# A state-space scan with side work planned into it: one product moved a step later, matmul allowance held back before GpSimd tiles, and two products per image moved from GpSimd to VectorE

## The chip, the cores and the metric

The kernel runs on one core of a Trainium2 chip. The core has a matmul engine (TensorE, PE), a vector engine (VectorE, DVE), an activation engine (ScalarE, ACT), a general-purpose engine (GpSimd, POOL) and SyncE (SP), which here only issues DMAs. Each engine runs its own instructions in order and waits for the others by semaphores. PE writes to PSUM, a small memory that DVE and ACT can read[...]. The metric is the device time of one execution in microseconds (us).

## What is computed

The input x is 8 images of 64 x 64 pixels with 96 channels. The first layer is a normalisation, two projections, a 3 x 3 depthwise convolution, and then a selective scan over all 4096 pixels of an image in four directions, whose results are added and gated. The second layer is a multilayer perceptron between an up- and a downsampling, written as matrix products. Nearly all the time belongs to the scan:

```python
K, D_INNER, D_STATE = 4, 192, 16
def step(h, inp):
    ul, dl, Bl, Cl = inp
    dA = jnp.exp(dl[..., None] * A)
    h = dA * h + (dl * ul)[..., None] * Bl[:, :, None, :]
    y = jnp.einsum('bkdn,bkn->bkd', h, Cl)
    return (h, y)
_, ys = lax.scan(step, h0, (u_t, d_t, B_t, C_t))
return y + xs * Dk[None, :, :, None]
...
y = (y1 + y2 + y3 + y4)
```

For each of 192 channels and 16 states there is one recurrence h = dA * h + (dl * u) * B along the pixels. The sum over the 16 states of h * C is y. The four directions k differ in the order in which they go through the pixels. All numbers are float32.

## The kernel before

**Tiles and chunks.** A tile is 8 channels with 16 states each, so 128 partitions, times 1024 pixels. 24 tiles make a chunk (all 192 channels of 1024 pixels), 4 chunks a direction, 4 directions (in the order k = 1, 0, 2, 3) an image, so an image has 16 chunks, c0 to c15, and the program 3072 tiles. The 24 tiles of a chunk fall into three thirds q of 8 tiles. Chunk c1 is the second chunk of direction k = 1.

**A tile's work**, in the order of dependence:

- `fetch` (L1020): a DMA on SP brings dl * u, spread over the 16 states, into `dub` (4 buffers).
- `product_b` (L1026): POOL multiplies it by B: `bb` (4 buffers).
- `decay` (L1032, L1039): PE spreads dl over the states into a PSUM tile `pd` (2 buffers), ACT takes the exp in place.
- `scan` (L1046): DVE runs the recurrence over `pd` and `bb`. The result goes back into `pd`, or, for a tile that has `by_pool` set, into `h` in SBUF[...].
- `product_c` (L1052): the product with C, on DVE, or on POOL for a tile with `by_pool`: every third tile of a chunk (tiles 2, 5, 8, ... 23).
- `hold` (L1065): the last state is copied into `carry` for the next chunk; on ACT for a tile with `by_pool`, on DVE otherwise. It is left out in a direction's last chunk.
- `sums` (L1084): for each pair of tiles, PE adds the 16 states up into the PSUM tile `py`, which gathers a whole third and has one buffer.

When a third is complete, one more PE product (L1096) adds to `py` what `before` has loaded as `yp`: for k = 1 it is u times a diagonal matrix of D, for k = 2 and 3 the result of an earlier direction. k = 0 has no such product. Then `store` copies `py` to `yq` on ACT (L1117) and, one turn later, writes it with two DMAs on SP (L1120).

**The order** of all engines' instructions is written out by hand (`tc.manual_schedule()`), one turn of the loop at L1143 per tile, called step i here, and counted within its chunk (0 to 23) in what follows. Step i issues, in this order: the load of `yp` if tile i is the fifth of its third (L1180), the fetch of tile i + 6, the POOL product C of tile i - 1 if that tile is POOL's, the product B of tile i + 3, the decay of tile i + 1, the scan of tile i with its DVE product C and its carry, then side work (`side.advance`, L1197), at times a filler matmul (`turn_over`, L1054), and in odd steps the sums of tiles i - 3 and i - 2. So the last sums of a third, and the product L1096 behind them, stand in steps 1, 9 and 17 of a chunk; those in step 1 belong to the last third of the chunk before.

**Side work** is all the rest: the first layer's front for the next image, the tail of the last image's scan, its multilayer perceptron, and for the next chunk the projections and dl (`prepare`). It is written as generators. Each piece says what it will cost before it is issued: us of an engine, KB of DMA, and PSUM banks. The planner, `Side`, gives each step an allowance per engine (L49: for PE 2.2 us, and with what is saved at most 2.9), and `emit` issues a piece only if its allowance is left. `advance` goes through stores, then urgent pieces, then the rest. Its argument `taken` is PE time that the step will use for itself: 0.95 us for a pair's sums and 0.95 for the product L1096. `turn_over` issues a filler matmul (L1058) when the step has spent less than 1.0 us of PE.

The parts of the side work that come up below are: `tail`'s sum of two directions on POOL (`ty`, L646), the upsampling copies on ACT (`t1s`, L769, two buffers) with their writes on SP (L775), and the load `u` (L933) with which `prepare` begins, in step 16 of most chunks.

Of the kernel before, what the change touches and what calls it, by code (L numbers as in the profile page):

```python
# [25 lines left out]
NT = DI // 8  # L26
# [11 lines left out]
class Side:  # L38
# [66 lines left out]
            active.append(entry)  # L105
        return True

    def advance(self, caps, more=1, spare=1, taken=0.0):

        self.caps, self.spent = caps, taken
        if caps:
            self.left = {e: min(self.left.get(e, 0.0) + c, most) for e, (c, most) in caps.items()}
            self.left["pe"] -= taken
        self.free += self.given
        self.given = []
        for active, spare_ in ((self.stores, 0), (self.hurried, 0), (self.active, spare)):  # L120
            for entry in list(active):
                if not self.emit(entry, spare_):
                    active.remove(entry)
            for _ in range(2):
                if self.urgent and active is self.hurried:
                    self.start(self.urgent, self.hurried, 0)
        for _ in range(more):
            if not self.queue or not self.start(self.queue, self.active, spare):
                break

    def drain(self):
        while self.stores or self.urgent or self.hurried or self.queue or self.active:
            self.advance(None, more=2)
# [3 lines left out]
def kernel(ctx: ExitStack, tc: tile.TileContext, a: dict, out: bass.AP):  # L137
    nc = tc.nc
# [13 lines left out]
    def load(name, shape, pool=cp):  # L152
        t = pool.tile(shape, F32, tag=name, name=name)
        queue().dma_start(t, a[name])
        return t

    ident = load("ident", [128, 128])
# [55 lines left out]
    d_diag = cp.tile([128, Q3, 128], F32, name="d_diag")  # L213
# [6 lines left out]
    with tc.tile_pool(name="ps0", bufs=1, space=PSUM) as ps0, tc.tile_pool(name="setup", bufs=1) as c0p:  # L220
# [76 lines left out]
        for quarter in range(2):  # L297
            grid = wave[:, cols[SIDE, quarter]]
            start, stop = quarter == 0, quarter == 1
# [4 lines left out]
                start=start,  # L304
                stop=stop,
                skip_group_check=True,
            )
        for quarter in range(2):
            grid = wave[:, cols[SIDE, quarter]]
            start, stop = quarter == 0, quarter == 1  # L310
# [50 lines left out]
    side = Side(pss)  # L361
# [636 lines left out]
    tiles = []  # L998
    for b in range(images):
        for k in (1, 0, 2, 3):  # L1000
            order = range(NCH) if k < 2 else range(NCH - 1, -1, -1)
            for n, c in enumerate(order):
                got = {}
                for i in range(NT):
                    q, n8 = divmod(i, 8)
                    s, j = n8 % 2, n8 // 2
                    tiles.append(
                        dict(b=b, k=k, i0=c * T, first=n == 0, i=i, q=q, s=s, j=j, g=8 * q + 4 * s + j, got=got)
                    )
                    tiles[-1]["last"] = n == NCH - 1  # L1010
                    tiles[-1]["by_pool"] = i % 3 == 2
    carry = pp.tile([128, NT], F32, tag="carry", name="carry", bufs=1)

    summed = set()
# [60 lines left out]
    def sums(two):  # L1075

        t0 = two[0]
        if t0["j"] == 0:
            t0["got"]["py"] = psy.tile([128, MB], F32, tag="py", name="py")
        py = t0["got"]["py"]  # L1080
        for t in two:
            for hf in range(2):
                r0 = 64 * hf + 32 * t["s"]
                nc.tensor.matmul(  # L1084
                    py[r0 : r0 + 32],
                    sel_r[:, t["j"], :],
                    t["hc"][:, MB * hf : MB * hf + MB],
                    start=(t["j"] == 0),
                    stop=(t["j"] == 3 and t["k"] == 0),
                    skip_group_check=True,  # L1090
                )

        if t0["j"] == 3 and t0["k"]:

            add = d_diag[:, t0["q"], :] if t0["k"] == 1 else ident
            nc.tensor.matmul(py, add, t0["got"]["yp"], start=False, stop=True, skip_group_check=True)  # L1096

    def before(t):

# [14 lines left out]
    def store(t):  # L1114
        yield dict(act=0.7)
        yq = sp.tile([128, MB], F32, tag="yq", name="yq", bufs=1)
        nc.scalar.copy(yq, t["got"]["py"])  # L1117
        yield {}
        for hf, part in enumerate(parts(t)):
            nc.sync.dma_start(part, yq[64 * hf : 64 * hf + 64])  # L1120
        if t["q"] == Q3 - 1:
            if t["k"] == 3:
                summed.add((t["b"], t["i0"] // T))
            elif t["k"] == 2 and t["i0"] == 0:
                summed.add((t["b"], "even"))
# [3 lines left out]
    with tc.manual_schedule():  # L1129
        side.queue, rest = front(0)  # L1130
        side.drain()
        side.urgent = prepare(0, tiles[0]["k"], tiles[0]["i0"], tiles[0]["got"])
        side.drain()
        n = len(tiles)
        for i in range(FETCH):
            fetch(tiles[i])
            if i >= FETCH - LEAD:
                product_b(tiles[i - FETCH + LEAD])
        decay(tiles[0])
        begin, *side.later = prepare(0, tiles[NT]["k"], tiles[NT]["i0"], tiles[NT]["got"])  # L1140
        side.urgent.append(begin)
        total = 1
        for i in range(n + 4):  # L1143
            t = tiles[i] if i < n else None
            at = i % (NT * NCH * K)
            if t and t["i"] == 0:
                b = t["b"]
                if at == 0:
                    y_dram[b] = [dr.tile([DI, L], F32, tag=f"y{o}", name=f"y{o}") for o in range(2)]
                    side.begun, hasty = 0, sum(item[1] for item in rest) if b == 0 else 0  # L1150
                    side.queue += rest
                    down, end = [], []
                    if b:
                        keep = {}
                        side.queue += tail(b - 1, keep)
                        up, down, end = mlp(b - 1, keep)
                        side.queue += up
                    if b + 1 < images:
                        start, rest = front(b + 1)
                        side.queue += start[:2] + [i for two in zip(down, start[2:10]) for i in two] if b else start[:10]  # L1160
                        side.queue += start[10:] + rest
                        rest = []
                    else:
                        side.queue += down
                    side.queue += end
                    total = sum(item[1] for item in side.queue)
                if b == images - 1 and at == NT * NCH * (K - 1):
                    keep = {}
                    side.queue += tail(b, keep, pairs=False)
                    total = 0  # L1170

            ahead = 4 if i < 2 * NT else 8
            if (i + ahead) % NT == 0 and i + ahead + NT < n:
                nxt = tiles[i + ahead + NT]
                begin, *side.later = prepare(nxt["b"], nxt["k"], nxt["i0"], nxt["got"])
                side.urgent.append(begin)
            if i % NT == 0:
                side.urgent += side.later
                side.later = []
            if t and t["i"] % 8 == 4:  # L1180
                before(t)
            if i + FETCH < n:
                fetch(tiles[i + FETCH])
            if 0 < i <= n and tiles[i - 1]["by_pool"]:
                product_c(tiles[i - 1])
            if i + LEAD < n:
                product_b(tiles[i + LEAD])
            if i + 1 < n:
                decay(tiles[i + 1])
            if t:  # L1190
                scan(t)
                if not t["by_pool"]:
                    product_c(t)
                hold(t)
            ends = i % 2 == 1 and 3 <= i <= n + 2
            adds = ends and tiles[i - 2]["j"] == 3 and tiles[i - 2]["k"]
            side.advance(  # L1197
                Side.CAPS,
                2 if not total or side.begun < max(hasty, total * at / 290) else 0,
                0 if 7 <= i % NT <= 21 else 1,  # L1200
                0.95 * (bool(ends) + bool(adds)),
            )
            turn_over()
            if ends:
                sums(tiles[i - 3 : i - 1])
                if tiles[i - 2]["j"] == 3:
                    side.stores.append([g := store(tiles[i - 2]), next(g)])
        up, down, end = mlp(images - 1, keep)
        side.queue += up + down + end
        side.drain()  # L1210
# [89 lines left out]
```

## Time and profile before

| | us |
|---|---|
| median of 3 runs | 11214.56 |
| lowest and highest of them | 11200.23, 11256.48 |
| the profiled execution's own time | 11227.57 |
| its span | 11225.8 |

The page's groups, each a line of the code on one engine, show what a tile costs:

| group | count | mean ns | idle before, us in total |
|---|---|---|---|
| L1026 POOL, product B | 3072 | 2359 | 254.7 |
| L1052 POOL, product C | 1024 | 2357 | 370.8 |
| L1052 DVE, product C | 2048 | 1225 | 157.2 |
| L1046 DVE, scan into pd, with carry | 1536 | 2350 | 287.7 |
| L1046 DVE, scan into h, with carry | 768 | 2339 | 7.8 |
| L1046 DVE, scan into pd, first chunks | 512 | 2291 | 149.5 |
| L1039 ACT, exp | 3072 | 1087 | 4592.7 |

Matmuls are better read from the timeline, where one merged row is a group of them: the decay of a tile is 1.13 us, the sums of a pair 1.07, the product L1096 1.13, a filler 1.13. "Idle before" is the time for which the engine did nothing before the rows of this group; it is a loss only where the engine is the one that sets the pace. In the timeline it stands in brackets behind the row, with the instruction that ended it: `[1.76 <-ACT carry L1065]` means that the engine had stood still for 1.76 us until an ACT instruction, by semaphore the one at L1065, released it. If several instructions of that engine end within a short time, the name may be that of a neighbour.

The first scan starts 142.5 us into the span, the last one ends at 10930.8; what follows is the multilayer perceptron of the last image. An image takes 1334 to 1360 us, most chunks take 79 to 92 us.

### The profile page before, as it was taken

Reading aid. Unit: us, or ns where it says so; the run is one execution under the profiler, and the core shown is the slowest. Engines: PE = TensorE matmul, PEld = TensorE weight load, DVE = VectorE, ACT = ScalarE, POOL = GpSimd, SP = SyncE. Lnnn points to the kernel's source line nnn. Section 1 sums busy time; section 2 is a strip of 40 time slices with the busy share of each in tenths; the row PEclk is TensorE's granted clock in tenths of the full one; section 3 lists DMA queues with packets and bytes.
Section 4 is the critical chain, followed back from the end, with each engine's and each line's share of the span. In section 5 each row is a group of like instructions: output and inputs, shape, how many; then the busy total and the mean of one; then the engine's idle time right before and its main releaser. Section 6 shows DMA issues by size and latency. Waiting matters only on the chain. (4 is left out here: it accounts for less than half of the span.)

```text
span 11225.8 us, 137177 instructions
## 1 busy us (share of the span) xinstructions
PE 10052.8 (90%) x45022; PEld 3217.9 (29%) x45022; DVE 10212.6 (91%) x7711; ACT 5906.0 (53%) x8218; POOL 10175.5 (91%) x4665
## 2 busy tenths in 40 slices
PE   7898888999889998899889998899988999889888
PEld 2222222322223222332223322233222332223224
DVE  5999999999999999999999999999999999999980
ACT  4455444656455564555545555455644656455443
POOL 4999999999999999999999999999999999999990
PEclk9999999999999999999999999999999999999998
DMA  5878898899988999888988989889898899988981
GB/s 145 220 201 224 211 232 206 215 225 234 230 206 217 230 231 226 209 221 222 236 213 215 222 215 246 206 216 225 221 240 207 216 225 232 231 208 215 224 198 41
DMA packets 1045102, 2401.26 MB, mean 214 GB/s; under 512 B 293948, under 2 KB 315708, under 8 KB 1044392
## 3 DMA queue, kind: packets, MB, share of 16 engines
q1 hardware_dynamic: 1040872, 2391.03, 85.8%
q8 instruction: 361, 5.91, 0.2%
q14 instruction: 349, 2.86, 0.1%
q10 hardware_dynamic: 3520, 1.46, 0.1%
HBM read 1929.05 MB, written 328.73 MB: 201 GB/s over the span
## 5 line engine op out<-in xcount | busy, mean ns | idle before, releaser
L1026 POOL TENSOR_TENSOR bb<-dub,br 128x1024 f32<-128x1024 f32 x3072 | 7174.5, 2359 | 254.7 <-DMA dub<-du 167.9
L1039 ACT ACTIVATE pd<-pd,neg_a 128x1024 f32<-128x1024 f32 x3072 | 3340.3, 1087 | 4592.7 <-PE pd L1032 4566.6
L1032 PE MATMUL pd<-dl,sel_b 64*128 64x512 f32 x12288 | 3528.3, 647 | 942.1 <-DVE carry L1065 625.6
L1046 DVE TENSOR_TENSOR_SCAN pd<-pd,carry,bb 128x1024 f32<-128x1024 f32 x1536 | 3610.1, 2350 | 287.7 <-ACT carry L1065 117.5
L1052 POOL TENSOR_TENSOR hc<-h,cr 128x1024 f32<-128x1024 f32 x1024 | 2413.9, 2357 | 370.8 <-DVE h L1046 303.1
L1052 DVE TENSOR_TENSOR hc<-pd,cr 128x1024 f32<-128x1024 f32 x2048 | 2508.1, 1225 | 157.2 <-PE py L1084 14.7
L1032 PEld LDWEIGHTS pd<-dl,sel_b 64*128 64x128 f32 x12288 | 967.7, 186 | 3230.9 <-issue 1534.8
L1046 DVE TENSOR_TENSOR_SCAN h<-pd,carry,bb 128x1024 f32<-128x1024 f32 x768 | 1796.2, 2339 | 7.8 <-ACT pd L1039 7.4
L1084 PE MATMUL py<-hc,sel_r 128*32 128x512 f32 x12288 | 1723.2, 620 | 34.6 <-POOL hc L1052 34.4
L1046 DVE TENSOR_TENSOR_SCAN pd<-pd,bb 128x1024 f32<-128x1024 f32 x512 | 1173.1, 2291 | 149.5 <-ACT pd L1039 68.7
L1058 PE MATMUL idle<-sel_b,ident 128*128 128x512 f32 x1654 | 949.4, 656 | 5.2 <-DVE ty L682 5.2
L524 PE MATMUL pc<-pad,convr 96*128 96x512 f32 (+1 forms) x2304 | 858.7, 614 | 2.0 <-issue 2.0
L1046 DVE TENSOR_TENSOR_SCAN h<-pd,bb 128x1024 f32<-128x1024 f32 x256 | 583.3, 2278 | 26.1 <-ACT pd L1039 24.3
L988 POOL TENSOR_TENSOR u<-dl,u 128x512 f32<-128x512 f32 x384 | 486.0, 1272 | 126.9 <-DMA br<-xd 126.7
L1084 PEld LDWEIGHTS py<-hc,sel_r 128*32 128x32 f32 x12288 | 251.1, 109 | 1115.3 <-issue 862.0
L821 PEld LDWEIGHTS p<-w2q,mq 128*100 128x100 f32 x4800 | 452.6, 168 | 274.5 <-issue 214.4
L814 PE MATMUL ph<-xu,w 96*128 96x500 f32 x960 | 505.7, 630 | 11.5 <-ACT mq L815 6.7
L821 PE MATMUL p<-w2q,mq 128*100 128x96 f32 x4800 | 511.1, 258 | 2.3 <-ACT mq L815 2.3
L944 PE MATMUL px<-u,xp 64*64 64x512 f32 x1536 | 427.4, 630 | 37.4 <-DMA u<-u 35.0
L1058 PEld LDWEIGHTS idle<-sel_b,ident 128*128 128x128 f32 x1654 | 252.9, 191 | 613.5 <-issue 575.5
L524 PEld LDWEIGHTS pc<-pad,convr 96*128 96x128 f32 (+1 forms) x2304 | 262.2, 162 | 561.5 <-issue 559.3
L969 PE MATMUL pv<-xd,dt_w 64*64 64x512 f32 x1536 | 398.5, 610 | 2.0 <-ACT xd L954 2.0
(153 smaller groups left out, 6763.1 us busy)
## 6 DMA issues: line engine op xcount, KB each, us to landing
dub<-du SPq DMA_DIRECT2D x3072, 512.0 KB
u<-u SPq DMA_DIRECT2D x256, 384.0 KB
du<-u SPq DMA_DIRECT2D x768, 128.0 KB
y<-yq SPq DMA_DIRECT2D x768, 128.0 KB
br<-xd SPq DMA_DIRECT2D x256, 256.0 KB
cr<-xd SPq DMA_DIRECT2D x256, 256.0 KB
yp<-y SPq DMA_DIRECT2D x384, 128.0 KB
yp<-u SPq DMA_DIRECT2D x192, 128.0 KB
```

The lines of the kernel that those rows point to most:

```text
L524: nc.tensor.matmul(t[rows].rearrange("p (i j) -> p i j", i=8), weights[:, cs], v["pad"][:, 8 * blk + kw : 8 * blk + kw + 8, kh : kh + H], ...
L814: nc.tensor.matmul(t[:, :px], w1[:, m, :], xu, start=True, stop=True)
L821: nc.tensor.matmul(t[:SIDE, C * i : C * i + C], sq[:, m, row], w2q[:, m, :], start=(m == 0), stop=(m == 2))
L944: nc.tensor.matmul(p[rows], xp[rows, k, q, :], v["u"][rows, q, :], start=(q == 0), stop=(q == 2), skip_group_check=True,)
L988: nc.gpsimd.tensor_tensor(v["u"][:, q, :], got["dl"][:, q, :], v["u"][:, q, :], ALU.mult)
L1026: nc.gpsimd.tensor_tensor(t["bb"], t["dub"], t["got"]["br"], ALU.mult)
L1032: nc.tensor.matmul(pd[:, MB * hf : MB * hf + MB], sel_b[rows, 4 * t["s"] + t["j"]].rearrange("p n c -> p (n c)"), t["got"]["dl"][rows, t[" ...
L1039: nc.scalar.activation(pd, pd, AF.Exp, scale=neg_a[:, t["k"], t["g"] : t["g"] + 1])
L1046: nc.vector.tensor_tensor_scan(t["h"][:, ::step], pd[:, ::step], t["bb"][:, ::step], 0.0 if t["first"] else held, ALU.mult, ALU.add)
L1052: (nc.gpsimd if t["by_pool"] else nc.vector).tensor_tensor(t["hc"], t["h"], t["got"]["cr"], ALU.mult)
L1058: nc.tensor.matmul(p, ident, sel_b[:, 0:4].rearrange("p j n c -> p (j n c)"), start=True, stop=True)
L1084: nc.tensor.matmul(py[r0 : r0 + 32], sel_r[:, t["j"], :], t["hc"][:, MB * hf : MB * hf + MB], start=(t["j"] == 0), stop=(t["j"] == 3 and t ...
```

## The change

Three edits:

1. The product L1096 leaves `sums` and becomes a function of its own, `add`. It is issued one step after the last sums of its third, at the end of that step (steps 2, 10 and 18 of a chunk), and the store of the third is queued after it, so one step later too. For k = 0, where there is no product, the store stays where it was. The allowance `taken` follows: 0.95 in a step with sums or with an `add`, where a step with both had 1.9.
2. `advance` has a new argument `eve`. In a step whose next tile is POOL's (from chunk 2 of the first image on), what is saved of the PE allowance over one step's 2.2 us is put aside before side work is issued and given back behind it.
3. In the second chunk of k = 1 (c1) of all images but the first, every fourth tile's product C is POOL's instead of every third's: tiles 3, 7, 11, 15, 19 and 23. Where a product moves, `scan` writes to `pd` instead of `h` and `hold` copies on DVE instead of ACT, or the reverse.

```diff
-    def advance(self, caps, more=1, spare=1, taken=0.0):
+    def advance(self, caps, more=1, spare=1, taken=0.0, eve=False):
+        kept = 0.0
         self.caps, self.spent = caps, taken
         if caps:
             self.left = {e: min(self.left.get(e, 0.0) + c, most) for e, (c, most) in caps.items()}
-            self.left["pe"] -= taken
+            if eve:
+                kept = max(0.0, self.left["pe"] - caps["pe"][0])
+            self.left["pe"] -= taken + kept
...
+        if kept:
+            self.left["pe"] += kept
...
+                busy = b and k == 1 and n == 1
...
-                    tiles[-1]["by_pool"] = i % 3 == 2
+                    tiles[-1]["by_pool"] = i % 4 == 3 if busy else i % 3 == 2
...
-        if t0["j"] == 3 and t0["k"]:
-
-            add = d_diag[:, t0["q"], :] if t0["k"] == 1 else ident
-            nc.tensor.matmul(py, add, t0["got"]["yp"], start=False, stop=True, skip_group_check=True)
+    def add(t):
+
+        to = d_diag[:, t["q"], :] if t["k"] == 1 else ident
+        nc.tensor.matmul(t["got"]["py"], to, t["got"]["yp"], start=False, stop=True, skip_group_check=True)
...
+        behind = None
...
-            adds = ends and tiles[i - 2]["j"] == 3 and tiles[i - 2]["k"]
+            third = tiles[i - 2] if ends and tiles[i - 2]["j"] == 3 else None
             side.advance(
                 Side.CAPS,
                 2 if not total or side.begun < max(hasty, total * at / 290) else 0,
                 0 if 7 <= i % NT <= 21 else 1,
-                0.95 * (bool(ends) + bool(adds)),
+                0.95 * bool(ends or behind),
+                2 * NT <= i < n - 1 and tiles[i + 1]["by_pool"],
             )
             turn_over()
             if ends:
                 sums(tiles[i - 3 : i - 1])
-                if tiles[i - 2]["j"] == 3:
-                    side.stores.append([g := store(tiles[i - 2]), next(g)])
+            if behind:
+                add(behind)
+            done = behind or (third if third and not third["k"] else None)
+            behind = third if third and third["k"] else None
+            if done:
+                side.stores.append([g := store(done), next(g)])
```

In the order of the built program, 14 products C, 14 scans and 14 carry copies change their place, 288 products and stores are a step later, there are 26 fewer fillers, and side work stands in other steps than before: in an image from the second on, for example, 46 side matmuls are in c1 instead of 63, and 92 in c3 instead of 78.

## The prediction

> **What bounds the kernel now.** I read three views in this order: the page's first section, then busy time in stretches of one chunk each (a chunk is 24 steps, a step is one tile; c1 is chunk 1 of an image), then the timeline where VectorE stands still.
>
> ```profile
> PE 10052.8 (90%) x45022; PEld 3217.9 (29%) x45022; DVE 10212.6 (91%) x7711; ACT 5906.0 (53%) x8218; POOL 10175.5 (91%) x4665
> ...
> 2905.00:2996.00 91.00, 77.67 (x337) 21.91 (x335) 82.04 (x67) 42.41 (x64) 90.91 (x45) 1.00 1.00 244
> ...
> 3175.00:3267.00 92.00, 75.54 (x334) 22.92 (x334) 77.19 (x64) 41.02 (x61) 78.98 (x37) 0.89 0.77 199
> ...
> 3835.00:3917.00 82.00, 81.66 (x332) 21.69 (x332) 78.59 (x63) 48.19 (x66) 78.77 (x37) 1.00 0.89 225
> ```
>
> The columns of a stretch are its length, then busy us of PE, weight loads, DVE, ACT, POOL, then PE clock, DMA share, GB/s. The first is c1 of image 2: POOL 90.91 of 91, so GpSimd bounds it. The second is c4: nobody is full, and the clock fell to 0.89. The third is c12: PE, DVE and POOL are all near full. Most chunks are like it, with 2.4 to 4 us of DVE idle, so DVE bounds the program, and only its waits can be won. Read scan by scan, the idle time before the scans is 57.5 us per image (images 1 to 7). Some 0.25 us at every scan behind a GpSimd tile is a floor: such a scan follows the last one without a product between.
>
> **Part 1, the add (288 products, one per third of k = 1, 2, 3).** What it takes away, in c1:
>
> ```profile
> 2913.22 2.34 DVE L1046 TENSOR_TENSOR_SCAN h<-pd,carry,bb 128x1024 f32<-128x1024 f32 x1
> 2913.90 1.13 PE L1096 MATMUL py<-yp,d_diag 128*128 128x512 f32 x2
> 2914.95 1.13 PE L1032 MATMUL pd<-dl,sel_b 64*128 64x512 f32 x4
> ...
> 2916.13 1.09 ACT L1039 ACTIVATE pd<-pd,neg_a 128x1024 f32<-128x1024 f32 x1 [4.02 <-PE pd L1032]
> ...
> 2917.32 2.36 DVE L1046 TENSOR_TENSOR_SCAN pd<-pd,carry,bb 128x1024 f32<-128x1024 f32 x1 [1.76 <-ACT carry L1065]
> ```
>
> The add stands before tile 3's decay matmuls; exp and scan 3 follow one another, and scan 3 has no product before it, since tile 2 is GpSimd's. Thirds end in steps 1, 9 and 17; behind steps 9 and 17 comes a tile whose scan has a DVE product in front, and no wait is seen there. In the twelve chunks whose step 1 has an add, the wait at scan 3 above the floor, counted to at most the add's 1.1 us and leaving c1 to part 3, is 4.25 us per image and 6.7 in image 0: 36 in all. Next late there is the scan before it or B, so I take **-34**.
>
> What it adds: py has one PSUM buffer. The copy yq of a third (L1117) used to run a step before the next third's first sums; now it is issued in the same step, behind that step's exp, and in step 11 also behind the carry copy, which waits for scan 11 to end. The sums wait for it, and on PE's queue stand behind them the decays of the next tile, then exp, then scan. c12, step 11, before:
>
> ```profile
> 3874.11 2.28 DVE L1046 TENSOR_TENSOR_SCAN h<-pd,bb 128x1024 f32<-128x1024 f32 x1
> ...
> 3876.43 0.19 ACT L1065 COPY carry<-h 128x1 f32<-128x1 f32 x1 [0.41 <-DVE h L1046]
> ...
> 3876.68 1.06 PE L1084 MATMUL py<-hc,sel_r 128*32 128x512 f32 x8
> 3877.68 1.13 PE L1032 MATMUL pd<-dl,sel_b 64*128 64x512 f32 x4
> ...
> 3878.91 1.09 ACT L1039 ACTIVATE pd<-pd,neg_a 128x1024 f32<-128x1024 f32 x1 [1.27 <-PE pd L1032]
> ...
> 3880.10 2.30 DVE L1046 TENSOR_TENSOR_SCAN pd<-pd,bb 128x1024 f32<-128x1024 f32 x1
> ```
>
> Carry ends at 3876.62; yq (0.59) and some 0.06 of signalling put the sums at 3877.27, 0.6 later than 3876.68. The chain from sums to scan 13 has 0.1 of air, so the scan is late by 0.5. I did this at every place: new PE wait minus PE's idle time before the next decay minus the air between exp and scan.
>
> - Step 3: wait 0.53, air 0.92; 3 us over the program.
> - Step 11: wait 0.78, air 0.73 on the mean, uneven; 30 us.
> - Step 19: wait 0.76, air 0.40; 39 us.
>
> Together 72. Where GpSimd is late anyway it costs nothing; I take **+65**. From below 15, if the planner's shifted side work opens air; from above the whole wait, 0.69 x 287 = 198.
>
> On SP the two y stores go behind the two yp loads and one dub fetch. At the end of c0 these four took 5.0 us of issue before the next fetch; split, no fetch waits for four. POOL's wait for dub is 167.9 us in 3072 products and seldom reaches a scan: 0. Uncovered, a fetch is later by two issues, 2.4 us.
>
> **Part 2, the eve.** No instruction is added. Up to 0.7 of saved PE allowance is kept from the step before a GpSimd tile and returned after it, so side matmuls move a step or two: in c1 17 fewer, in c3 14 more; before the next image the debt is paid. Fillers (L1058) fall from 1654 to 1602 records. Of the idle time before scans, 9.7 us per image is outside scan 3, c1, c4 and the floors, much of it from dub or a side DMA. A seventh of it: **-10**; ends +20 and -68.
>
> The shift reaches c4:
>
> ```profile
> 3249.08 0.58 ACT L769 COPY t1s<-p 100x512 f32<-100x512 f32 x1 [8.46 <-DMA t<-t1s]
> 3249.56 1.09 ACT L1039 ACTIVATE pd<-pd,neg_a 128x1024 f32<-128x1024 f32 x1
> ...
> 3250.75 2.30 DVE L1046 TENSOR_TENSOR_SCAN pd<-pd,bb 128x1024 f32<-128x1024 f32 x1 [7.26 <-ACT pd L1039]
> ```
>
> A copy into t1s (two buffers) waits for the write of the tile two before, issued at 3237.84: 11.2 us, behind the prepare load u, issued at 3235.47. The exp stands behind the copy. An earlier such write, issued at 3230.89, freed its tile at 3235.95, in 5.1. In the new order all twelve copies come about two steps later: the first two tiles' writes are issued right behind u and take the long landing, but the fifth tile's copies have a step (some 3.5 us) after the write they wait for, where they had none. One stall grows by up to 6, the other shrinks by up to 7, and the wait at scan 15 (1.3) loses its cause. I take -2.5 of 11 us per image: **-18**; ends -45 and +45. Here the Trainium skill (TensorE: Matmul & The Clock Gate, Part 1, What's actually happening) says that about 3.4 us without matmuls halve the PE clock. The trace agrees: PE idles 4.95 us here, the chunk's clock is 0.89, and the decays after it take 2.08 us instead of 1.13; scans 21 and 22 then wait 1.03 and 0.48. By the row the sum is -18; by the rule, if PE's pause fell under 3.4 us, those waits less floor would go too, 1.26 x 7 = 9 more. I take none: a pause of that length remains. The new waits of part 1 are under 1.1 us and reach no such window.
>
> **Part 3, chunk 1 of images 1 to 7.** Fourteen products leave POOL (2357 ns each) for DVE (1225, and a carry copy of 148 that ACT did): per image POOL -4.7, DVE +2.75. The scans wait 1.47, 1.93, 2.45 and 2.24 us at tiles 0, 3, 9 and 12, all in the first half. Ahead of B for tile 12 POOL has two products instead of three: 2.36 sooner. In the second half DVE waits for nobody and carries one product more: +1.37. That leaves -1.0; C 7 now comes one step before its sums, where C 8 had two, so I take -0.7 x 7 = **-5**. Ends: -18 (POOL's bound opens until DVE is full) and +19 (14 x 1.37, nothing returned).
>
> **The end.** After the last decay, 712 program matmuls instead of 707, and the last stores a step later: **+2**.
>
> **Sum:** -34 + 65 - 10 - 18 - 5 + 2 = 0. The profiled execution's own time is 11227.6 (span 11225.8); the median shown is 11214.6, 13 lower, and its runs lie from 11200 to 11256. I put the time between: **11222**. Half a per cent, 56 us, is about what a measurement of this kernel can tell from no change.
>
> **Rivals.**
>
> - *Copy absorbed.* The wait for yq costs 15 and c4 gives -45: -34 + 15 - 10 - 45 - 5 + 2 = -77, **11150**. For it: PE's order loosens in the eve steps. Against: the copy is timed by DVE's scan and exp, not by PE, so a freer PE only waits longer.
> - *Copy uncovered* (the other side). Each wait reaches the scan: 198 - 67 + 2 = +133, **11361**. Place: sums of steps 3, 11 and 19; price 0.69 each. It decides from (56 + 65) / 287 = 0.42 per third. For it: c12 and c13 have no PE slack. Against: the air at step 3.
> - *Collision.* In c4 both landings take the long time: +45 instead of -18, **11285**. For it: u goes out one step before. Against: the step of slack gained.
> - *Chunk 1 opens.* -18 instead of -5, 11209; same class as the forecast.
>
> **Chances.** No change 0.48 (its own range 11165 to 11270; chunk 1's rival in it), copy absorbed 0.22, copy uncovered 0.20, collision 0.10. So faster 0.22, same 0.48, slower 0.30. The range, 11120 to 11310, leaves out most of the uncovered case.
>
> **What would show it.** Scan 3's idle time in chunks with an add down to some 0.3 (part 1's gain); a wait of PE's L1084 sums for ACT's yq, some 0.7 us about 285 times, and new idle time at scans 13 and 21 (its cost); c1 between 88.5 and 91 us, its first half shorter and its second longer; c4's longest scan wait cut or moved to tile 19 or 20. I am wrong if scans 13 and 21 stay at their old idle time, or if c4's stall is gone altogether.

## The result, and the profile after

| | before | after |
|---|---|---|
| median, us | 11227.96 | 11237.25 |
| lowest to highest, us | 11200.23 to 11256.48 | 11214.98 to 11253.93 |
| runs | 12 | 12 |
| profiled execution's own time, us | 11227.57 | 11214.98 |
| its span, us | 11225.8 | 11213.2 |

The ratio is **1.0009, 95% interval 1.0000 to 1.0018**: no change that can be measured. The profile shown of after is of the execution with the lowest of its twelve times. Its last scan ends at 10937.0 us, 6.2 later than before, and its span is shorter only because what follows takes 276.2 us where it took 295.0; over the kept profiles this last stretch has one of two lengths, 271 to 277 us (after, e8, e11, e12) at a granted clock of 0.90 to 0.92, or 291 to 301 us (all others) at 0.80 to 0.83. So the two spans are not compared as wholes; they are compared place by place, and us per image are means over images 1 to 7.

The page's first section of after (busy us, count) and its group of the sums (busy, mean ns, idle before):

```profile
PE 9994.5 (89%) x44970; PEld 3209.9 (29%) x44970; DVE 10255.7 (91%) x7739; ACT 5903.1 (53%) x8204; POOL 10147.3 (90%) x4651
...
L1092 PE MATMUL py<-hc,sel_r 128*32 128x512 f32 x12288 | 1700.0, 616 | 210.0 <-ACT yq L1125 129.2
```

The same group before:

```profile
L1084 PE MATMUL py<-hc,sel_r 128*32 128x512 f32 x12288 | 1723.2, 620 | 34.6 <-POOL hc L1052 34.4
```

The sums' idle time on PE was 34.6 us, nearly all of it waiting for POOL's product C; now it is 210.0, and 129.2 of it ends with the copy yq. The view of waits has the same as a count (us in total, times, longest):

```profile
PE py L1092 <- ACT yq L1125: 129.2, 183, 1.1
```

So 0.71 us each. By their times in the trace, 281 of the 287 sums that stand behind such a copy start within 0.25 us of its end; where they are not among the 183, the wait is put down to another engine or hardly shows as idle time.

The gain is seen at scan 3. Steps 2 and 3 of c11, image 2, where only edits 1 and 2 act, first before, then after:

```profile
3760.34 2.34 DVE L1046 TENSOR_TENSOR_SCAN h<-pd,carry,bb 128x1024 f32<-128x1024 f32 x1
3760.52 1.13 PE L1096 MATMUL py<-yp,ident 128*128 128x512 f32 x2
3761.58 1.13 PE L1032 MATMUL pd<-dl,sel_b 64*128 64x512 f32 x4
...
3763.95 2.36 DVE L1046 TENSOR_TENSOR_SCAN pd<-pd,carry,bb 128x1024 f32<-128x1024 f32 x1 [1.27 <-ACT pd L1039]
```

```profile
3764.17 2.34 DVE L1054 TENSOR_TENSOR_SCAN h<-pd,carry,bb 128x1024 f32<-128x1024 f32 x1
3764.40 1.13 PE L1040 MATMUL pd<-dl,sel_b 64*128 64x512 f32 x4 [0.48 <-DVE hc L1060]
...
3766.76 2.36 DVE L1054 TENSOR_TENSOR_SCAN pd<-pd,carry,bb 128x1024 f32<-128x1024 f32 x1 [0.25 <-ACT pd L1047]
3767.21 1.02 PE L1104 MATMUL py<-yp,ident 128*128 128x512 f32 x2
```

Before, the add stands ahead of the decay of tile 3, which starts 1.24 us after scan 2 does, and scan 3 waits 1.27. After, the decay starts 0.23 behind the start of scan 2, scan 3 waits 0.25, the floor, and the add comes behind it. (In c1, the place that the prediction shows, tile 2 is no longer POOL's after the change, and scan 3 doesn't wait at all; there edits 1 and 3 can't be told apart.)

The cost is seen at scans 13 and 21, two scans behind the step in which a third's first sums stand. Step 11 of c14, image 2, first before, then after:

```profile
4040.10 2.34 DVE L1046 TENSOR_TENSOR_SCAN h<-pd,carry,bb 128x1024 f32<-128x1024 f32 x1
...
4042.67 1.06 PE L1084 MATMUL py<-hc,sel_r 128*32 128x512 f32 x8
...
4044.90 1.09 ACT L1039 ACTIVATE pd<-pd,neg_a 128x1024 f32<-128x1024 f32 x1 [1.21 <-PE pd L1032]
...
4046.09 2.36 DVE L1046 TENSOR_TENSOR_SCAN pd<-pd,carry,bb 128x1024 f32<-128x1024 f32 x1
```

```profile
4047.42 2.34 DVE L1054 TENSOR_TENSOR_SCAN h<-pd,carry,bb 128x1024 f32<-128x1024 f32 x1
...
4049.79 0.19 ACT L1073 COPY carry<-h 128x1 f32<-128x1 f32 x1 [0.55 <-DVE h L1054]
4049.89 0.58 ACT L1125 COPY yq<-py 128x512 f32<-128x512 f32 x1
...
4050.57 1.07 PE L1092 MATMUL py<-hc,sel_r 128*32 128x512 f32 x8 [0.53 <-POOL bb L1034]
4051.56 1.13 PE L1040 MATMUL pd<-dl,sel_b 64*128 64x512 f32 x4
...
4052.80 1.09 ACT L1047 ACTIVATE pd<-pd,neg_a 128x1024 f32<-128x1024 f32 x1 [1.30 <-PE pd L1040]
...
4053.99 2.36 DVE L1054 TENSOR_TENSOR_SCAN pd<-pd,carry,bb 128x1024 f32<-128x1024 f32 x1 [0.59 <-ACT pd L1047]
```

Before, the sums start 2.57 us after scan 11 does, and scan 13 is 5.99 behind scan 11, with no wait. After, ACT copies carry, then yq, which ends at 4050.47; the sums start at 4050.57, 3.15 after scan 11, and scan 13 is 6.57 behind it. (The bracket of the sums names POOL; by the times it is yq that ended last. A wait for several semaphores is put down to one of them.) 0.58 us of ACT work on a 53% busy engine has become 0.59 us of idle time on the engine that sets the pace.

Idle time before scans, us per image, at the places the prediction named:

| place | before | after |
|---|---|---|
| all scans | 57.5 | 54.3 |
| scan 3, chunks with an add, without c1 | 7.35 | 2.94 |
| scan 13 | 0.39 | 3.28 |
| scan 21 | 4.18 | 7.17 |

What scan 3 gives, 4.4, scans 13 and 21 take back and more, 5.9. The scans' lower total is no gain in time: an image takes 1353.0 us on the mean where it took 1350.8, and edit 3 alone gives DVE 2.75 us more work in it. The chunks of edits 2 and 3, in the view of stretches (columns as in the prediction; c1, then c4 of image 2):

```profile
2902.24:2994.32 92.08, 80.63 (x316) 21.86 (x310) 85.66 (x71) 42.51 (x60) 87.81 (x43) 0.94 1.02 249
3176.48:3268.13 91.65, 75.25 (x334) 22.88 (x334) 79.03 (x65) 41.45 (x60) 77.91 (x38) 0.91 0.75 200
```

In c1, on the mean of the seven images, POOL lost 3.2 us of work (4.7 moved away, side work came in) and DVE got 2.9, but the chunk is not shorter: 92.2 us where it was 91.8. Scan to scan, its first half (to scan 12) went from 46.68 to 45.75 us and its second from 45.07 to 46.45. POOL, with 87.81 of 92.08 us, does not fill the chunk any more; the time it left is taken by new stalls. The longest of image 2 is at tile 11, again in the timeline:

```profile
2939.98 1.92 PE L1092 MATMUL py<-hc,sel_r 128*32 128x512 f32 x4 [2.00 <-POOL hc L1060]
...
2941.83 1.85 PE L1040 MATMUL pd<-dl,sel_b 64*128 64x512 f32 x4
...
2943.73 1.09 ACT L1047 ACTIVATE pd<-pd,neg_a 128x1024 f32<-128x1024 f32 x1 [6.67 <-PE pd L1040]
...
2944.92 2.35 DVE L1054 TENSOR_TENSOR_SCAN h<-pd,carry,bb 128x1024 f32<-128x1024 f32 x1 [3.01 <-ACT pd L1047]
```

With half of a pair's sums done, PE waits 2.00 us for a product C of POOL. The other half then takes 1.92 us, where a whole pair takes 1.07, and the decay behind it 1.85 instead of 1.13; exp and scan 11 come after that.

c4 went from 91.0 to 91.4 us although its scans wait less (12.44 to 10.96): the waits at scans 15 and 17 (1.32 and 1.22) are gone, but the long one at tile 19 is still there (6.77 to 6.48), and DVE does 1.7 us more of side work in this chunk (79.0 for 77.3; with edit 1 alone it is 78.9).

### The profile page after: what moved, and what is told of

Its sections match the earlier page's. It is cut to its first block, busy times and chain, and to the rows that moved or that the text cites. A ratio compares the mean times of both kernels' runs of the same rounds, so it can differ in the third digit from the quotient of the medians.

```text
span 11213.2 us, 137194 instructions
## 1 busy us (share of the span) xinstructions
PE 9994.5 (89%) x44970; PEld 3209.9 (29%) x44970; DVE 10255.7 (91%) x7739; ACT 5903.1 (53%) x8204; POOL 10147.3 (90%) x4651
## 5 line engine op out<-in xcount | busy, mean ns | idle before, releaser
L1060 POOL TENSOR_TENSOR hc<-h,cr 128x1024 f32<-128x1024 f32 x1010 | 2381.3, 2358 | 454.8 <-DVE h L1054 354.1
L1092 PE MATMUL py<-hc,sel_r 128*32 128x512 f32 x12288 | 1700.0, 616 | 210.0 <-ACT yq L1125 129.2
L1054 DVE TENSOR_TENSOR_SCAN h<-pd,carry,bb 128x1024 f32<-128x1024 f32 x754 | 1764.5, 2340 | 29.5 <-ACT pd L1047 25.9
L1066 PE MATMUL idle<-sel_b,ident 128*128 128x512 f32 x1602 | 903.6, 646 | 4.1 <-DVE ty L688 3.6
```

What stands on the lines that cost most here:

```text
L1054: nc.vector.tensor_tensor_scan(t["h"][:, ::step], pd[:, ::step], t["bb"][:, ::step], 0.0 if t["first"] else held, ALU.mult, ALU.add)
L1060: (nc.gpsimd if t["by_pool"] else nc.vector).tensor_tensor(t["hc"], t["h"], t["got"]["cr"], ALU.mult)
L1066: nc.tensor.matmul(p, ident, sel_b[:, 0:4].rearrange("p j n c -> p (j n c)"), start=True, stop=True)
L1092: nc.tensor.matmul(py[r0 : r0 + 32], sel_r[:, t["j"], :], t["hc"][:, MB * hf : MB * hf + MB], start=(t["j"] == 0), stop=(t["j"] == 3 and t ...
```

## The experiments

Twelve kernels, each timed against the kernel before. In the expectations, theory A is the prediction's own account with its sizes; F is the rival that edit 1 helps by taking the y stores out of a busy place on SP's queue; J is the rival that chunk 1 loses because each of POOL's products C comes in the second tile of its pair, one step before the sums that need it. A hundredth of a per cent is 1.1 us. All ratios are to before.

| run | what it is | ratio | 95% |
|---|---|---|---|
| e1 | edit 1 alone | 0.9982 | 0.9972 to 0.9992 |
| e2 | edit 2 alone | 0.9994 | 0.9985 to 1.0003 |
| e3 | edit 3 alone | 1.0026 | 1.0019 to 1.0033 |
| e9 | edits 1 and 2 | 0.9994 | 0.9985 to 1.0002 |
| e4 | after, copy at once | 0.9955 | 0.9943 to 0.9968 |
| e6 | before, copy at once | 0.9996 | 0.9986 to 1.0006 |
| e8 | edits 1 and 2, copy at once | 0.9959 | 0.9947 to 0.9971 |
| e5 | before, y stores a step later | 1.0006 | 0.9998 to 1.0013 |
| e7 | edit 3 alone, first tile of a pair | 0.9996 | 0.9988 to 1.0004 |
| e10 | after, copy at once, first tile of a pair | 0.9919 | 0.9906 to 0.9931 |
| e11 | before, three t1s buffers | 0.9965 | 0.9952 to 0.9977 |
| e12 | e10 with three t1s buffers | 0.9888 | 0.9873 to 0.9902 |

### The three edits one by one

e1 is after with `False` for `eve` and `i % 3 == 2` everywhere; e2 is before with the argument `eve` and what it does in `advance`; e3 is before with the two lines of `busy`; e9 is after without those two.

> The kernel before with the first edit alone: the product that adds to a third's sums one step later, its store too, allowance as in the change. Theory A (gain and price of this edit cancel): scan 3 loses some 4.5 us of idle time per image, scans 13 and 21 together gain some 6, PE's sums wait for the copy yq some 130 us in all; so the time is +12 us, ratio 1.001, between 0.999 and 1.004. Rival B (the waits at scans are interchangeable, since GpSimd and DMA are as full as VectorE, and what is won or lost at a scan comes back within the chunk): ratio 1.000 and chunk lengths as before. Rival C (the edit is a clean gain and the other two give it back): ratio 0.997.

> The kernel before with the second edit alone: saved matmul allowance held back in the step before a GpSimd tile. Theory A: a small gain, mostly in c4, where the upsampling copies come in another order of steps (the fifth tile's copies keep a step between them and the write they wait for), and at scans behind GpSimd tiles in c11: -20 us, ratio 0.998, between 0.995 and 1.001. Rival B: 1.000. Rival C (this edit gives back what the first wins): 1.002 or more.

> The kernel before with the third edit alone: in c1 of images 1 to 7 every fourth tile's product C on GpSimd instead of every third's. Theory A: c1's first half is shorter by some 2 us, its second longer by 1.4; -5 us in all, ratio 0.9995, between 0.998 and 1.001. Rival D (GpSimd's bound opens in the whole chunk): c1 2.6 us shorter, -18 us, 0.998. Rival C: 14 products of 1.37 us are simply added to VectorE, +19 us, 1.002.

> The changed kernel without its third edit (the copy out of PSUM at its place in the changed kernel). If the three edits add up (0.9982, 0.9994 and 1.0026 alone): ratio 0.9976. If the third edit is worth its cost only in the order that the other two make, as the pair of runs with the early copy says (0.9955 with it, 0.9959 without): 1.001, as the changed kernel, between 1.000 and 1.002.

The sum of the prediction, taken apart, fails in all three terms. Edit 1 alone was to cost 31 us (-34 + 65) and gains 20. Edit 2 was to gain 28 (the eve and c4) and gains 7, which is not told from nothing. Edit 3 was to gain 5 and costs 29. None of the ratios named for e1 came: it lies outside theory A's range and nearest to C's. The three single results add to +2 us, after itself is +10. They don't add pair by pair: edits 1 and 2 together give -7 where the two alone give -27, so with edit 1 in place the eve costs some 13 us (with the two intervals, -1 to 28), and edit 3 on top of both costs 17 (3 to 30). That also lies between the two forecasts for e9. The errors were large and of both signs, and cancelled.

A reason why edits 1 and 2 don't add is in their traces: they win the same waits. us per image at three scans (scan 3 in chunks with an add, without c1):

| scan | before | e1 | e2 | e9 |
|---|---|---|---|---|
| 3 | 7.35 | 2.56 | 3.62 | 2.47 |
| 0 | 5.85 | 2.67 | 3.75 | 3.99 |
| 12 | 6.56 | 3.60 | 2.34 | 3.10 |

In e2 the add stands where it stood, and half of scan 3's wait is gone all the same: between the decays of tiles 2 and 3 PE had 2.14 us of side matmuls and fillers on the mean before, and has none in e2. The prediction had left scan 3 out of what the eve could win. In e2 as a whole nothing is won by it: its scans wait 57.7 us per image, before 57.5, since other chunks lose as much (c4 waits 13.5 instead of 12.4).

In e1's trace the predicted moves are there: scan 3 waits 5.5 us per image less, scans 13 and 21 wait 2.3 and 5.2 more, and the waits view has the price in the same size as after:

```profile
PE py L1092 <- ACT yq L1125: 134.3, 185, 1.7
```

What was not foreseen in this size is a gain in c0, c1, c3, c10 and c11, 1.9 to 2.4 us in each, some 10.5 per image. Their scans wait 8.3 less, of which scan 3 has 3.8 and scans 0 and 12 have 5.7. The other chunks give most of it back, 8.7 per image (c4 2.5, c12 1.8).

### The price of the copy

In e4 the copy into yq does not wait for the store's turn; it is issued on ACT in the same step as the product, behind it. Nothing else changes its place on any engine.

```diff
+    def copy(t):
+        t["yq"] = sp.tile([128, MB], F32, tag="yq", name="yq", bufs=1)
+        nc.scalar.copy(t["yq"], t["got"]["py"])
...
-        yq = sp.tile([128, MB], F32, tag="yq", name="yq", bufs=1)
-        nc.scalar.copy(yq, t["got"]["py"])
+        if not t["k"]:
+            copy(t)
+        yq = t["yq"]
...
             if behind:
                 add(behind)
+                copy(behind)
```

> The changed kernel with one thing moved: the copy of a third out of PSUM (yq, for k = 1, 2, 3) is issued on ScalarE directly behind the added product, not in the next step behind that step's exp and carry copy. All other engines' orders are those of the changed kernel, instruction by instruction. Theory A (the price of the first edit is the wait of the next third's sums for this copy): PE's wait for yq nearly goes, idle time at scans 13 and 21 falls by 5 to 6 us per image, -45 us against the changed kernel, ratio to the kernel before 0.997, between 0.995 and 0.999. Rival B (waits interchangeable): as the changed kernel, 1.001. Rival E (scans 13 and 21 are late for another reason, as the shifted product or side work before their decays): PE's wait for yq goes, and the scans' idle time and the time stay, 1.001.

The ratio falls from 1.0009 to 0.9955, by 0.0054, that is 61 us (with the two intervals, some 43 to 79), where the prediction had priced the uncovered part of the copy at 65. The same step 11 of c14 in e4's timeline:

```profile
4028.28 0.58 ACT L1124 COPY yq<-py 128x512 f32<-128x512 f32 x1 [0.81 <-PE py L1104]
...
4029.16 2.34 DVE L1054 TENSOR_TENSOR_SCAN h<-pd,carry,bb 128x1024 f32<-128x1024 f32 x1
...
4031.53 0.19 ACT L1073 COPY carry<-h 128x1 f32<-128x1 f32 x1 [0.55 <-DVE h L1054]
...
4031.70 1.07 PE L1092 MATMUL py<-hc,sel_r 128*32 128x512 f32 x8
...
4035.13 2.36 DVE L1054 TENSOR_TENSOR_SCAN pd<-pd,carry,bb 128x1024 f32<-128x1024 f32 x1
```

yq stands in idle time of ACT, before scan 11 begins; the sums are back at 2.54 us after the scan, scan 13 is 5.97 behind it, as before the change (5.99). Over the program the sums' wait for yq is gone from the view of waits, and scans 13 and 21 wait 1.57 and 4.11 us per image, the second as before the change. With scan 5, which step 3's wait reaches (0.93 in after, 0 in e4), that is 5.7 us per image less than in after, some 46 in all; the last scan of this profile is 39 us earlier than after's (10898.4 against 10937.0). The rest, up to the 61, is not located.

That an early copy is of use by itself was the rival. The control puts it into before, straight behind the product there:

```diff
             if ends:
                 sums(tiles[i - 3 : i - 1])
                 if tiles[i - 2]["j"] == 3:
+                    if tiles[i - 2]["k"]:
+                        copy(tiles[i - 2])
```

> A control: the kernel before, with the copy of a third out of PSUM (k = 1, 2, 3) issued directly behind the added product, which stays where it was, in the same step as the last sums. Theory A (an early copy is worth what it takes from the wait of the next sums): the kernel before has no such wait, since its copy stands a step ahead of those sums, so the ratio is 1.000, between 0.999 and 1.001. Rival H (an early copy is worth something by itself, on ScalarE's queue): 0.996, as the gain of the same move in the changed kernel.

It does nothing (0.9996, the interval holds 1). So what e4 wins is the price that the later product puts on a late copy, not a gain that was to be had anyway. e8 is the same copy in edits 1 and 2, without edit 3:

> The first two edits with the copy out of PSUM directly behind the added product, and without the third edit. If the parts add up (0.9955 with all three, 1.0026 for the third alone): ratio 0.993, -80 us, between 0.9915 and 0.9945. If the third edit's loss is in the end the same wait as the copy's and was won back with it: 0.9955.

Against its own base e9 it gains 0.0035, 39 us (22 to 56): less than the 61, but the two intervals overlap. It also ends level with e4, where e9 was 17 us below after, so that with the copy at once edit 3 costs nothing that can be measured.

### Is edit 1's extra gain SP's queue?

```diff
     def store(t):
...
         nc.scalar.copy(yq, t["got"]["py"])
         yield {}
+        yield {}
```

> The kernel before with one thing moved: the two DMAs that write a third's result (y) are issued one step later, so that on SyncE's queue they stand behind the two loads of yp and one fetch of dub instead of ahead of them. The added product, its place and the copy out of PSUM stay. Theory F (the first edit gains not only at scan 3 but by this place on SyncE's queue, which the prediction put at 0: GpSimd's wait for dub fell from 168 to 106 us with it): GpSimd's wait for dub falls by 40 to 60 us, idle time at scans 0 and 12 falls, -25 us, ratio 0.998, between 0.9965 and 0.999. Rival G (all of the first edit's gain is the product's new place on TensorE): ratio 1.000 and GpSimd's wait for dub as before.

1.0006, interval 0.9998 to 1.0013: no gain, so F falls. (The stores of k = 0, which the change leaves in place, are later here too.) POOL's wait for dub, which F would have had fall by 40 to 60 us, is 163.7 us for 167.9 before. It does fall in e1 (106.1) and in e2 (129.9), and e2 doesn't move the stores. The prediction's 0 for the reordering on SP holds. Neither the store's place nor the copy's explains e1's extra gain. One thing goes with it: the PE clock granted over the span was 0.980 to 0.984 in every run of e1, and 0.972 to 0.978 in every run of before beside it; of the five chunks that gain in e1 four have a clock higher by 0.02, and the fifth by 0.01. PE stands still for 1.5 us or more 82 times between the first and the last scan of e1's profile, and 182 times before; the last section shows that such pauses go ahead of a lower clock. Whether the higher clock makes the chunks shorter, or the shorter stalls keep the clock up, these runs do not tell, and clock and time don't go together everywhere: after has 0.976 to 0.979 and e4 0.976 to 0.978, some 61 us apart. In e1 the side work also stands in other steps, since `taken` is 0.95 where it was 1.9; that was not tried alone. This stays open.

### Why chunk 1 gained nothing

Two products per image is the net of edit 3: in c1 six tiles leave POOL (2, 5, 8, 14, 17 and 20) and four come to it (3, 7, 15 and 19). e7 is e3 with one number changed: POOL gets the first tile of a pair (2, 6, 10, ...), two steps before the pair's sums, instead of the second (3, 7, 11, ...), one step before.

```diff
-                    tiles[-1]["by_pool"] = i % 4 == 3 if busy else i % 3 == 2
+                    tiles[-1]["by_pool"] = i % 4 == 2 if busy else i % 3 == 2
```

> The third edit alone, but with GpSimd's products in c1 at tiles 2, 6, 10, 14, 18 and 22 instead of 3, 7, 11, 15, 19 and 23. Count and cost on every engine are the same. Each of these products has two steps before the sums that need it, where tiles 3, 7, 11 and so on have one. Theory J (the third edit loses 30 us because the sums wait for a GpSimd product that is only one step ahead, and the next decay and VectorE's buffers of products stand behind them): the wait at scans 9 and 11 and before VectorE's product 8 goes, ratio 1.000, between 0.999 and 1.001. Rival K (VectorE's 14 added products and the full DMA queue in c1 are the whole loss): 1.0026 as with the odd tiles.

1.0026 becomes 0.9996: the one step is worth 0.0030, 34 us (22 to 46). c1 is 93.3 us long in e3 and 90.0 in e7, before has 91.8; the halves are 46.89 and 46.40 in e3, 43.51 and 46.49 in e7. DVE's idle time in c1 tells the same: 10.2 us before, 8.8 in e3, 5.2 in e7, where the moved products cost it 2.75 of work. So 3.3 us in each of seven chunks, 23 in all, are in c1, and in its first half. The two profiles, whose spans are 42 us apart, differ by as much again in c0, c10 and c11 (0.9, 1.5 and 0.9 us per image), where no product is moved; why, was not looked into. How the wait arises, in the timeline of e3, tiles 3 and 4 of image 2:

```profile
2926.00 2.35 POOL L1053 TENSOR_TENSOR hc<-h,cr 128x1024 f32<-128x1024 f32 x1
...
2927.76 1.70 PE L1085 MATMUL py<-hc,sel_r 128*32 128x512 f32 x8
...
2928.40 0.14 PEld L1085 LDWEIGHTS py<-hc,sel_r 128*32 128x32 f32 x4 [0.50 <-POOL hc L1053]
...
2929.46 1.13 PE L1033 MATMUL pd<-dl,sel_b 64*128 64x512 f32 x4
```

POOL's product for tile 3 runs to 2928.35. PE has begun the pair's sums, does the half that belongs to tile 2, and must stop for the half of tile 3 until POOL is done; the decay behind it starts at 2929.46. Counted over the seven chunks, a tile's sums start within less than 0.3 us of the end of POOL's product, so PE was there first or nearly so, at 13 of 42 products in e3 (all seven of tile 3, six of tile 7) and at 5 of 42 in e7 (tile 6). Before it is 22 of 56 (tiles 5, 8 and 11), so that by this count alone e3 is no worse than before. The stall itself is larger than that wait. The rows up to scan 9 in e3:

```profile
2934.40 1.13 PE L1033 MATMUL pd<-dl,sel_b 64*128 64x512 f32 x4 [2.76 <-DVE carry L1066]
...
2939.12 1.94 PE L1085 MATMUL py<-hc,sel_r 128*32 128x512 f32 x8
...
2940.99 1.74 PE L1033 MATMUL pd<-dl,sel_b 64*128 64x512 f32 x4
2941.09 1.22 DVE L1053 TENSOR_TENSOR hc<-pd,cr 128x1024 f32<-128x1024 f32 x1 [1.73 <-PE py L1085]
...
2943.96 2.36 DVE L1047 TENSOR_TENSOR_SCAN pd<-pd,carry,bb 128x1024 f32<-128x1024 f32 x1 [1.58 <-ACT pd L1040]
```

PE stood still for 2.76 us, and afterwards sums take 1.94 us instead of 1.06 and a decay 1.74 instead of 1.13; DVE waits 1.73 for a free hc and 1.58 for the exp. The pause of 2.76 us ended with DVE, not with POOL's product, so this stall is not J's wait itself; after's stall at tile 11, shown above, is (2.00 us for POOL's product), and has the same slow decay (1.85). J's ratio came (1.000, between 0.999 and 1.001), so the place in the pair is worth what J said. How much of it is the wait and how much the slow rows that follow a pause was not taken apart, and e7 also ends on tile 22 instead of 23, which goes with the step.

### What the stall of c4 was worth

```diff
-            s = bp.tile([SIDE, 2, MB], F32, tag="t1s", name="t1s")
+            s = bp.tile([SIDE, 2, MB], F32, tag="t1s", name="t1s", bufs=3)
```

> The kernel before with three buffers instead of two for the upsampling copies (t1s). By the prediction's reading of c4 the long wait there is that of a copy for the write of the tile two before, with the exp behind it: with three buffers it goes, c4 of images 1 to 7 is 8 to 10 us shorter, -60 us, ratio 0.9945, between 0.993 and 0.997. If the time is only pushed on (the writes still take their landing, and the rows that are read back from them come no sooner): 0.999 or more.

The result is 0.9965, 39 us, less than was expected (0.9945). In the view of waits ACT's wait for such a write falls from 95.2 us in all to:

```profile
ACT t1s L769 <- DMA t<-t1s: 49.3, 15, 7.2
```

c4 shrinks from 91.0 to 86.6 us, half of the 8 to 10 expected: the 6.77 at tile 19 are gone, and 3.77 stand at tile 20 instead. So the write that frees t1s caused at least this part of the stall. It is not the whole account of the 39 us: c4 has 31 in seven images, other chunks give 20 back (c2 1.4 per image), and of the 37 us between the two profiles 21 lie behind the last scan, a stretch that is as short in after and e8, which have two buffers.

### All of it together

> The changed kernel with the copy out of PSUM directly behind the added product, and GpSimd's products in c1 at tiles 2, 6, 10 and so on. If the even tiles are worth here what they are alone (0.9996 against 1.0026): ratio 0.993, between 0.9915 and 0.9945. If the odd tiles' loss is hidden in this order by other waits: 0.9955.

> The early copy, the even tiles in c1 and three buffers of t1s together, on the changed kernel. If they add up: 0.993 x 0.996, ratio 0.989, between 0.986 and 0.992, -120 us. If they win the same waits twice: 0.993.

e10 takes the whole change, with the copy at once and POOL's product in the first tile of a pair: 0.9919. Against e4 this is the step of lead once more, worth 0.0036, 40 us (20 to 60), where e3 and e7 gave 34. e12 adds the third t1s buffer: **0.9888, 0.9873 to 0.9902**, a median of 11104.8 us, faster than both kernels. Its first section shows why it is not the amount of work:

```profile
PE 9923.9 (89%) x44970; PEld 3195.7 (29%) x44970; DVE 10237.1 (92%) x7739; ACT 5921.8 (53%) x8204; POOL 10145.2 (91%) x4651
```

DVE is 25 us busier than before the change, in a span that is 129 us shorter (11096.7; 105 up to the last scan, 24 behind it); its scans wait 41.6 us per image instead of 57.5.

## Why the prediction was right, and where it was not

The forecast, no change at 11222 us, stands: 11237.25, 15 above it. By its steps:

- **The bound.** DVE is full and only its waits can be won: right. e4, e11 and e12 leave its work about as it was and gain 0.35 to 1.1%.
- **The add taken away, -34.** Right in place and size: 4.4 us per image at scan 3 where 4.25 had been read, and 4.8 in e1. The eve alone takes 3.7 us there too (e2). And it was not all of edit 1. e1 holds a further gain of about 50 us (-20 measured against +31), some of it at scans 0 and 12, where the sum had nothing; its cause stays open.
- **The copy uncovered, +65.** Right: 61 measured (43 to 79), and 39 (22 to 56) without edit 3. The chain from yq to sums, decay, exp and scan is in the trace as it was told, with 0.71 us a wait against 0.69. The view names 183 waits where some 285 were forecast, and by their times 281 sums start right behind the copy. Read off the scans it is 5.9 us per image at scans 13 and 21, some 47 in all, and 0.9 at scan 5.
- **The stores on SP, 0.** Right (e5).
- **The eve, -10, and c4, -18.** Too much: -7 alone and about +13 on top of edit 1, neither told from nothing. In c4 the step "the other shrinks by up to 7" failed. The one at tile 19 gave up 0.3 in after, and side work that moved in took the rest. The waits at scans 15 and 17 went in after, but not in e2 (0.68 and 1.39), whose c4 is 1.4 us longer than before: it was not the eve alone that took them.
- **Chunk 1, -5.** Wrong in sign: +29 alone, +17 in after. c1 was to be 88.5 to 91 us and is 92.2. The second half came as worked out (+1.38 us per image against +1.37, +1.33 in e3). The first half failed: "Ahead of B for tile 12 POOL has two products instead of three: 2.36 sooner" gave 0.93 in after and nothing in e3. The sentence about C 7, one step before its sums, had the right mechanism and priced it at 0.3 us per image; by e3 and e7 the step is worth 34 us in all, of which 3.3 per image in c1. It was priced as one short wait of PE, and not for the decay behind it on PE's queue and the slow rows after a pause.
- **The end, +2.** Not tested: the stretch behind the last scan varies by some 20 us from profile to profile (see above).
- **The clock.** The working would have let two waits in c4 go if PE's pause there fell under 3.4 us. Behind shorter pauses the clock fell as well, as the last section counts, so that limit was not the right one.

So the total was right because a missed gain of some 50 us in edit 1 met misses of 21 and 34 us on the other side and a loss in putting the parts together. Two terms of edit 1 had their mechanism and size right; that the sum of all ended so near zero was luck. Of the rivals, the copy absorbed (11150) falls with the waits seen at scans 13 and 21, and so does the copy uncovered (11361): about a third of 198 us or less reached the scans, as the air at step 3 had it. The collision in c4 didn't come in after.

## What to carry to other kernels

When a product into a buffer that exists once is moved later, move the copy that empties it along, to the first idle place behind the product: here that was worth 61 us (39 without edit 3), and left behind it undid the gain. On a queue that runs in order, give a slow engine's product to the tile whose consumer is farthest away; one more step of lead was worth 34 us, in an edit that was to bring 5. And measure the edits of a change one by one even where the sum comes out as forecast.

## What was not expected of the hardware

After PE has stood still for 2 to 3 us the same matmuls can take nearly twice as long: in e3, one decay after the idle time of 2.76 us, every row is slow, and the sums of a pair take 1.94 us instead of 1.06. So a wait that costs DVE nothing when it happens can be paid for some tiles later. The clock granted to PE has only two levels in this kernel's records, full and half. Between the first and the last scan of the kernel before, 83 stretches at half clock begin, each some 3.4 us long or a multiple of that. Counted by PE's pauses in the same trace, leaving out one that fell into such a stretch (a stretch can stand behind two pauses):

| pause of PE, us | how many | a stretch at half clock begins in it or within 3.4 us behind it |
|---|---|---|
| 1.0 to 1.5 | 223 | 11 |
| 1.5 to 2.0 | 122 | 40 |
| 2.0 to 2.5 | 37 | 21 |
| 2.5 to 3.4 | 16 | 14 |
| over 3.4 | 7 | 7 |

So in this kernel a lower clock is often seen behind pauses of 1.5 us and more, the oftener the longer they are, and 3.4 us is no limit below which a pause is free.

In chunk 1 the clock may have decided the matter, though no run sets it apart: c1's mean granted clock is lower by 0.02 in after than in before, where it got 0.4 us longer, and higher by 0.02 in e1 and e7 and by 0.03 in e10, where it got 1.8 to 2.3 us shorter.
